# Last network of a four-stage kernel: seven block products for eight in two of four column blocks, and rows kept in DRAM

## Chip, cores, metric

One core of a Trainium2 chip. The metric is device time in microseconds (us) of one execution; several runs are made and the median is taken. Engines: PE (TensorE; PEld is its weight load), DVE (VectorE), ACT (ScalarE), POOL (GpSimd), SP (its queue issues most of the DMAs).

## What is computed

x is 8 x 256 rows of 512 values in float32. Four stages, each added to x: a long convolution over heads, a first gated network with 8-bit activations and ternary weights (hidden width 1408), an attention over the context, and a last gated network with 8-bit activations in groups of 64 and 1-bit weights (hidden width 2048). Cut to the two networks:

```python
def _bitlinear(x, w):                      # first network: one scale per row
    return jnp.einsum('bsi,oi->bso', _activation_quant(x), _weight_quant(w))
...
def _quant_weight_1b(w):                   # last network
    return _ste(w, jnp.sign(w) * jnp.mean(jnp.abs(w)))
def _quant_act(x):                         # groups of 64
    xg = x.reshape(shp[:-1] + (shp[-1] // GSIZE, GSIZE))
    s = jnp.clip(jnp.max(jnp.abs(xg), axis=-1, keepdims=True), EPS, None)
    q = jnp.round(jnp.clip(xg * (QB / s), -QB, QB)) * (s / QB)
    return _ste(x, q.reshape(shp))
def _bitlinear(x, w):
    return _quant_act(x) @ _quant_weight_1b(w).T
h = jax.nn.silu(_bitlinear(x, w1)) * _bitlinear(x, w2)
return _bitlinear(h, w3)
...
x = x + jnp.tanh(g_ffn[0]) * _L0_ffn_ref(_layernorm(x), ...)
x = x + jnp.tanh(g_xattn[1]) * _L1_xattn_ref(_layernorm(x), ctx_2048, ...)
x = x + jnp.tanh(g_ffn[1]) * _L1_ffn_ref(_layernorm(x), ...)
```

## The kernel before

The 2048 rows are 16 row tiles of 128 (`NT`), kept in SBUF as `xs`. Every engine works its instructions off in the order in which they are written: the program is under a manual schedule, so a step that waits holds up all that stands behind it on the same engine or queue.

*Convolution* (line 349 and around it, heads in a loop of 32): PE with float32 matmuls, DVE and POOL form products; `job(h, slot, ...)` hangs other work on the heads. Statistics for the layer normalisation of the first row tiles of the next stage are such jobs (`first_by_act`).

*First network* (loop over `t`, lines 861 to 1040): per row tile three column blocks of up products (`up_block`, L861), SiLU on ACT, a gate on DVE, then the row maximum (`row_max`), integers on ACT (`i8h`, L1018), clipping on POOL (`qh`, L1036), a transposing DMA (`hqT`, L1038), and two tiles later the 11 down products (`down0`, L878). `ln_finish` turns the statistics of four tiles into a reciprocal root on DVE and POOL; the group of the tiles 4 to 7 is done at `t == 1` (`FINISH[0]`). `odd_back` (L990, L991) adds what the convolution left over.

*Attention* (loop over `t` with `masked`, `readout`): PE float32, and SP loads keys, values and the last network's weights, of which ACT takes the signs.

*Last network.* The weights are +1 and -1 in `w1q[0]`, `w1q[1]` (512 x 2048 each) and `w1q[2]` (2048 x 512). An activation tile is split into a rounded part `hi` (ACT, L1163) and the rest `lo` (DVE, L1168), both fp32r, and both are multiplied. Per row tile, four column blocks of 512: `up_products` does 16 matmuls of 128x128 by 128x512 (two weights, hi and lo, four chunks of 128), then SiLU on ACT and the gate on DVE (`up_gate`, L1201). Two column blocks make a half of 1024 (`half_quantised`): group maximum (L1116), scale and reciprocal (L1128, L1130), a 32x32 transpose of the scales (L1329) and their way to DRAM (`d`, L1331), the integers `times` (L1135), their transposing DMA (`qT`, L1352), and the scales spread over the partitions from DRAM (`sT`, L1339, two issues). `hidden_high` then forms v = qT * sT on DVE (L1373) and its `hi`; `low` its `lo`. `down` does 32 matmuls a row tile (L1383), one row tile behind the up products. `front_turned` prepares the next row tile in the same way (normalisation L196, maximum, integers, DMAs, and v at L1433); `finish` adds the result to `xs` (L228) and stores it (L1396). Four PSUM banks take the up products in turn (`ps_mm`), two the down products (`ps_o`).

Of the kernel before, what the change touches and what calls it, by code (L numbers as in the profile page):

```python
# [13 lines left out]
I16 = mybir.dt.int16  # L14
# [28 lines left out]
def flamingo_gated_kernel(  # L43
# [65 lines left out]
    gw = const.tile([P, 2], F32, name="gw")  # L109
    gw0, gw1 = gw[:, 0:1], gw[:, 1:2]  # L110
# [534 lines left out]

    means = ((25, "act2"), (26, "act2"), (28, "act2"), (29, "act"))
# [228 lines left out]
    def down0(hqT):  # L875
        po = ps_o.tile([P, L], F32, tag="o", name="po")
        for c in range(NF0):
            nc.tensor.matmul(  # L878
                po, hqT[:, c, :], w0q[2][:, c, :], start=(c == 0), stop=(c == NF0 - 1)
            )  # L880
        return po


    natural = list(range(NT))
# [8 lines left out]
        0: (st0, 1, "0"), 4: (st0, 2, "0"), 8: (st0, 3, "0"),  # L893
# [103 lines left out]
    for t in range(NT + 1):  # L997
# [3 lines left out]
        if new and t > 0 and t != 2:  # L1001
            front_norm(t + 2)
# [11 lines left out]
        if t in (0, 2):  # L1014
            front_norm(t + 2)
        if 1 <= t:
            q = p1.tile([P, FF0], I8, tag="i8h", name="i8h")
            nc.scalar.activation(q, h_.pop(t - 1), AF.Copy, scale=sc)  # L1018
# [15 lines left out]
        if 1 <= t:  # L1034
            b = p2.tile([P, FF0], BF16, tag="qh", name="qh0")
            nc.gpsimd.tensor_scalar(b, q, 127.0, -128.0, ALU.min, ALU.max)  # L1036
            bT = p_hq.tile([P, NF0, P], BF16, tag="hqT", name="hqT")
            nc.sync.dma_start_transpose(out=bT, in_=b)  # L1038
            f3 = small.tile([P, 1], F32, tag="f3", name="f3")
            nc.gpsimd.tensor_scalar(f3, inv, gw0, None, ALU.mult)  # L1040
            hq_[t - 1] = (bT, f3)
# [8 lines left out]
        if t == 1:  # L1050
            ln_finish(*FINISH[0])
# [70 lines left out]
    def scales(v, n, tag, back=None):  # L1122

        back = group_max(v, n, tag, back)
        return back, to_8_bits(back, tag)

    def to_8_bits(back, tag):
        nc.vector.tensor_scalar(back, back, Q_EPS, 1.0 / 127.0, ALU.max, ALU.mult)  # L1128
        r = small.tile([P, back.shape[-1]], F32, tag="gr" + tag, name="gr")
        nc.vector.reciprocal(r, back)  # L1130
        return r
# [39 lines left out]
    def split(pool, v, tag):  # L1171
        return low(pool, v, high(pool, v, tag), tag)
# [27 lines left out]
    def up_gate(hh, pb, sl):  # L1200
        nc.vector.scalar_tensor_tensor(  # L1201
            hh, pb, wmean1[:, 1:2], sl, op0=ALU.mult, op1=ALU.mult
        )

    SIGNS = [2, 2, 2, 2, 2, 2, 2, 2, 2, 2, 1, 1, 1, 1]
    BY_POOL = set(range(4, NT))
    e_, r_ = {}, {}
    signs = [(0, make) for make in signs]  # L1210
    for t in range(NT + 2):
# [71 lines left out]
        if t == NT:  # L1283
            mean_w1(2)
            nc.vector.tensor_scalar(gw1, wmean1[:, 2:3], gate_f[1], None, ALU.mult)
# [8 lines left out]
        if t == NT - 2:  # L1294
            times(xn4, q, back)
        if t == NT - 1:
            ln_some(st4, natural, GRP, "4")
            hh = px.tile([P, FF1 // 2], F32, tag="hh", name="hh4")
# [10 lines left out]
    with ExitStack() as ph:  # L1309
        p2 = pool(ph, "p4", 2, reuse_waits="tile")  # L1310
        p3 = pool(ph, "p4three", 3, reuse_waits="tile")
        pk = pool(ph, "p4keep", 1, reuse_waits="tile")

# [7 lines left out]
        p1 = pool(ph, "p4one", 1, reuse_waits="tile")  # L1321
        NB = FF1 // 512
        HW = FF1 // 2
        HC, HG = HW // P, HW // GS

        def squares(back, tag):

# [9 lines left out]

# [6 lines left out]
        def half_quantised(hh, k):  # L1344

            back = backs["h", k]
            r = scales(hh, HW, "h", back[:, :HG])[1]
            d = squares(back, "h")
            q = p2.tile([P, HW], I16, tag="qh", name="qh")
            times(q, hh, r)  # L1350
            qT = p3.tile([P, HC, P], I16, tag="qT", name="qT4")
            nc.sync.dma_start_transpose(out=qT, in_=q)  # L1352
            sT = p3.tile([P, HC, P], F32, tag="sT", name="sT")
            spread_rows(sT, d, HC)
            return qT, sT

        def front_turned(t):

            back = backs["x", t % 2]
            xn, q = front(t, back[:, : L // GS])[:2]  # L1360
            d = squares(back, "x")
            qT = pk.tile([P, NL, P], I16, tag="xT", name="xT4")
            nc.sync.dma_start_transpose(out=qT, in_=q)
            sT = pk.tile([P, NL, P], F32, tag="xsT", name="xsT")
            spread_rows(sT, d, NL)
            return xn.rearrange("p (c m) -> p c m", m=P), qT, sT

        def hidden_high(halves, f):

            qT, sT = halves[f // 2]  # L1370
            c = slice((f % 2) * NL, (f % 2 + 1) * NL)
            v = p2.tile([P, NL, P], F32, tag="v", name="v4")
            nc.vector.tensor_tensor(v, qT[:, c, :], sT[:, c, :], ALU.mult)  # L1373
            return v, high(p1, v, f"h{f}")

        def hidden_parts(halves, f):
            return low(p1, *hidden_high(halves, f), f"h{f}")

        def down(po, hT, blocks):
            for b in blocks:  # L1380
                for c in range(NL):
                    for k in range(2):
                        nc.tensor.matmul(  # L1383
                            po,
                            hT[b][k][:, c, :],
                            w1q[2][:, b * NL + c, :],
                            start=(b == 0 and c == 0 and k == 0),
                            stop=(b == NB - 1 and c == NL - 1 and k == 1),
                        )

        def new_out():
            return ps_o.tile([P, L], F32, tag="o", name="po4")

        def finish(t, po):
            residual(t, po, gw1)
            nc.sync.dma_start(out=out[t * P : (t + 1) * P, :], in_=xs[:, t, :])  # L1396

        first, second = range(NB // 2), range(NB // 2, NB)
        prev, sums = None, []
        for t in range(NT):
            last = t == NT - 1
            for s in sums:
                finish(*s)
            sums, hT, high_ = [], [], {}
            if 0 < t < NT - 1:
                nxt = front_turned(t + 1)
            if t > 0:  # L1410
                hh = px.tile([P, HW], F32, tag="hh", name="hh4")
                g = up_products(xT, 0)
                if prev is not None:
                    high_ = {f: hidden_high(prev, f) for f in first}
                up_gate(hh[:, 0:512], *g)
                hT += [low(p1, *high_[f], f"h{f}") for f in first if f in high_]
                g = up_products(xT, 1)
                if prev is not None and not last:
                    high_ = {f: hidden_high(prev, f) for f in second}
                up_gate(hh[:, 512:1024], *g)  # L1420
            halves = [half_quantised(hh, 0)]
            if prev is not None and not last:
                hT += [low(p1, *high_[f], f"h{f}") for f in second]
            hh = px.tile([P, HW], F32, tag="hh", name="hh4")
            g = up_products(xT, 2)
            if t == 0:
                turned = front_transposed(xn4)
            up_gate(hh[:, 0:512], *g)
            if t == 0:
                nxtT = split(pk, turned, "x1")  # L1430
            g = up_products(xT, 3)
            if 0 < t < NT - 1:
                nc.vector.tensor_tensor(*nxt, ALU.mult)  # L1433
            if t + GRP + 1 < NT:
                ln_some(st4, natural, t + GRP + 1, "4")
            up_gate(hh[:, 512:1024], *g)
            if 0 < t < NT - 1:
                nxtT = split(px1, nxt[0], "x")
            xT = nxtT
            halves.append(half_quantised(hh, 1))  # L1440
            if 0 < t < NT - 1:
                po = new_out()
                down(po, hT, first if t == NT - 2 else range(NB))
                if t < NT - 2:
                    sums.append((t - 1, po))
                else:
                    begun = (po, hT)
            if last:
                po, hT0 = begun
                down(po, hT0, second)  # L1450
                hT += [hidden_parts(prev, f) for f in second]
                finish(t - 2, po)
                po = new_out()
                down(po, hT, range(NB))
                hT = [hidden_parts(halves, f) for f in range(NB)]
                finish(t - 1, po)
                po = new_out()
                down(po, hT, range(NB))
                finish(t, po)
            prev = halves  # L1460
# [47 lines left out]
```

## Time and profile before

| | |
|---|---|
| runs | 727.43, 728.82, 724.93 us; median 727.43 |
| profiled execution | 726.16 us, span 724.3, mean granted clock 0.995 |
| PE | 3200 instructions; up products of the last network: pa and pb, hi and lo, x256 each, 389 to 392 ns from start to modelled end |
| last network | from about 368 us to the end |
| last matmul, then residual and store | residual starts at 720.40 |
| DMA | 99.36 MB, mean 137 GB/s |

PE's matmuls are pipelined: the time from the start of one to the start of the next is shorter than the duration that a row shows. Where an engine waited, a line ends in brackets: how long it was idle, and what ended that.

### The profile page before, as it was taken

How to read it: one execution, taken by the hardware profiler on the slowest of the kernel's cores; microseconds unless marked ns; L12 is line 12 of the kernel's file. 1: busy time of each engine (PE TensorE's matmuls, PEld its weight loads, DVE VectorE, ACT ScalarE, POOL GpSimd, SP SyncE). 2: the span in 40 equal slices, each digit the busy share in tenths (PEclk: the TensorE clock that was granted, in tenths of full speed). 3: DMA queues.
4: the chain of work that ended last, by engine and by line, in shares of the span. 5: the costliest groups of instructions: out<-in, count | busy, mean ns of one | idle time of the engine just before them, and what ended most of it. 6: DMA issues, size and time to landing. Idle time of an engine off the chain costs nothing.

```text
span 724.3 us, 10121 instructions
## 1 busy us (share of the span) xinstructions
PE 711.4 (98%) x3200; PEld 531.6 (73%) x3200; DVE 598.5 (83%) x1224; ACT 367.4 (51%) x664; POOL 264.2 (36%) x371
## 2 busy tenths in 40 slices
PE   7999999999989999999999999999999999999997
PEld 6777777777544444657678888888888888888885
DVE  5699888999788887877877988988888988777965
ACT  5577887879787777757742222332222332212322
POOL 4798998989885535545400020000200002000000
PEclk8999999999999999999999999999999999999999
DMA  6675586921246566698605654454544454544443
GB/s 197 227 230 173 186 280 187 303 67 44 43 82 140 145 140 171 150 275 259 206 1 101 123 119 100 96 117 91 126 104 98 98 117 92 125 105 100 95 90 87
DMA packets 149970, 99.36 MB, mean 137 GB/s; under 512 B 83806, under 2 KB 127838, under 8 KB 149918
## 3 DMA queue, kind: packets, MB, share of 16 engines
q1 hardware_dynamic: 149608, 98.38, 52.3%
q0 software_dynamic: 256, 0.26, 0.6%
q8 instruction: 25, 0.41, 0.2%
q14 instruction: 27, 0.22, 0.1%
q10 hardware_dynamic: 54, 0.08, 0.1%
HBM read 75.58 MB, written 5.03 MB: 111 GB/s over the span
## 4 chain that ended last, share of the span: by engine, by line
PE 91%; DVE 2%; DMA 2%; POOL 2%; issue 1%; ACT 1%; SPq 0%; DVEq 0%; ACTq 0%; POOLq 0%
PE y L349 22%; PE po L1383 16%; PE pb L1189 15%; PE pa L1189 15%; PE po L878 5%; PE pa L861 4%; PE pb L861 4%; PE po L981 4%; PE ps L952 3%; PE tr L416 1%; PE tr L941 1%; DMA hqT<-qh 1%; DMA sT<-d 1%; DMA ch<-in_ctx_heads 1%; POOL xs L991 0%
## 5 line engine op out<-in xcount | busy, mean ns | idle before, releaser
L349 PE MATMUL y<-kv,toep 128*128 128x288 f32 x640 | 160.8, 408 | 0.7 <-ACT qx L313 0.6
L349 PEld LDWEIGHTS y<-kv,toep 128*128 128x128 f32 x640 | 119.9, 191 | 33.1 <-ACT qx L313 0.8
L1197 ACT ACTIVATE sl<-pa,wmean 128x512 f32<-128x512 f32 x64 | 44.0, 688 | 195.3 <-PE pa L1189 195.3
L1383 PE MATMUL po<-w,lo 128*128 128x512 f32 x256 | 99.9, 390 | 0.0
L1383 PE MATMUL po<-w,hi 128*128 128x512 f32 x256 | 99.6, 389 | 0.0
L181 POOL TENSOR_TENSOR nwt<-rstd 128x4 f32<-128x4 f32 x33 | 6.5, 198 | 242.2 <-DVE rstd L176 240.5
L326 POOL TENSOR_TENSOR kv<-cx 128x1024 f32<-128x1024 f32 x32 | 60.6, 1894 | 24.1 <-ACT cx L313 23.9
L1189 PE MATMUL pa<-w,hi 128*128 128x512 f32 x256 | 69.2, 392 | 0.0
L1189 PE MATMUL pb<-w,hi 128*128 128x512 f32 x256 | 68.6, 390 | 0.1
L1189 PE MATMUL pa<-w,lo 128*128 128x512 f32 x256 | 68.4, 389 | 0.0
L1189 PE MATMUL pb<-w,lo 128*128 128x512 f32 x256 | 68.4, 389 | 0.0
L394 POOL TENSOR_TENSOR prod<-prod 128x1024 f32<-128x1024 f32 x28 | 66.3, 2368 | 0.0
L861 PEld LDWEIGHTS <-xqT 128*128 128x128 bf16 x384 | 37.5, 98 | 37.8 <-issue 0.5
L1163 ACT CAST hi<-v 128x512 fp32r<-128x512 f32 x64 | 39.1, 622 | 48.2 <-DVE v L1373 48.1
L1201 DVE SCALAR_TENSOR_TENSOR hh<-pb,wmean,sl 128x512 f32<-128x512 f32 x64 | 47.7, 746 | 14.7 <-PE pb L1189 14.6
L1383 PEld LDWEIGHTS po<-w,lo 128*128 128x128 f32 x256 | 48.1, 188 | 10.9 <-DVE lo L1168 1.0
L1189 PEld LDWEIGHTS pa<-w,hi 128*128 128x128 f32 x256 | 47.8, 188 | 10.7 <-ACT hi L1163 0.6
L1189 PEld LDWEIGHTS pb<-w,hi 128*128 128x128 f32 x256 | 48.0, 188 | 10.5 <-DVE hh L1201 0.6
L1189 PEld LDWEIGHTS pa<-w,lo 128*128 128x128 f32 x256 | 48.1, 188 | 10.1
L1189 PEld LDWEIGHTS pb<-w,lo 128*128 128x128 f32 x256 | 48.1, 188 | 10.0
L1383 PEld LDWEIGHTS po<-w,hi 128*128 128x128 f32 x256 | 48.1, 188 | 9.9
L371 DVE TENSOR_TENSOR prod<-y,qx 128x512 f32<-128x512 f32 x64 | 43.7, 683 | 8.5 <-ACT y L359 4.4
(163 smaller groups left out, 1341.7 us busy)
## 6 DMA issues: line engine op xcount, KB each, us to landing
sT<-d SPq DMA_DIRECT2D x64, 256.0 KB
toep<-ssm_skip SPq DMA_DIRECT2D x31, 256.0 KB
ch<-in_ctx_heads SPq DMA_DIRECT2D x32, 128.0 KB
w1a<-in_L_w1t SPq DMA_DIRECT2D x8, 512.0 KB
w1a<-in_L_w2t SPq DMA_DIRECT2D x8, 512.0 KB
w1st<-in_L_w1t SPq DMA_DIRECT2D x16, 256.0 KB
w1st<-in_L_w2t SPq DMA_DIRECT2D x16, 256.0 KB
cT<-in_ctx_t SPq DMA_DIRECT2D x8, 512.0 KB
```

The source lines that it names most:

```text
L326: nc.gpsimd.tensor_tensor(kv[:, :, 0 : ND * HD].rearrange("p a (i d) -> p a i d", d=ND), cx[:, :, 0:HD].unsqueeze(3).to_broadcast([P, NL * ...
L349: nc.tensor.matmul(y[:, k, :, W0 : W0 + NPAIR], toeps[h][:, d * P : (d + 1) * P], kvs[h][:, mi * B : (mi + 1) * B, :].rearrange("p b n -> ...
L371: nc.vector.tensor_tensor(prod[:, 0, r, :, :], yv[:, :, W0 : W0 + ND * HD].rearrange("p a (i d) -> p a i d", d=ND), view(q, [HX, n], [1, H ...
L394: nc.gpsimd.tensor_tensor(flat[0], flat[0], flat[1], ALU.add)
L861: nc.tensor.matmul(pp[:, :fw], xqT[:, c, :], w0q[i][:, c, f0 : f0 + fw], start=(c == 0), stop=(c == NL - 1),)
L878: nc.tensor.matmul(po, hqT[:, c, :], w0q[2][:, c, :], start=(c == 0), stop=(c == NF0 - 1))
L981: nc.tensor.matmul(po, eT[:, c, :], cN[:, c, :], start=(c == 0), stop=(c == S // P - 1))
L1163: nc.scalar.copy(hi, v)
L1189: nc.tensor.matmul(pp, xT[k][:, c, :], w1q[i][:, c, f0 : f0 + 512], start=(c == 0 and k == 0), stop=(c == NL - 1 and k == 1),)
L1197: nc.scalar.activation(sl, pa, AF.Silu, scale=wmean1[:, 0:1])
L1201: nc.vector.scalar_tensor_tensor(hh, pb, wmean1[:, 1:2], sl, op0=ALU.mult, op1=ALU.mult)
L1383: nc.tensor.matmul(po, hT[b][k][:, c, :], w1q[2][:, b * NL + c, :], start=(b == 0 and c == 0 and k == 0), stop=(b == NB - 1 and c == NL - ...
```

## The change

In the last network, row tiles from 2 on are taken in pairs. For the first two of the four column blocks (`NS = 2`), the products of the pair's two row tiles with both weights are done as one 2 x 2 block product: the rows of the block matrix are the two row tiles, its inner index is the two halves of the 512 inputs (`KH = 2` chunks), its columns are the two weights. Seven block products of 4 matmuls (`plan_crossed`) take the place of eight, with four sums of activations (`sum_rows`, POOL, split into hi and lo again) and four combined weight forms for each column block (`t1` to `t4`, POOL, made once; `t1` in place of the second weight's first half). The seven results are put together on ACT, DVE and POOL. The other two column blocks are done as before (`plan_gated`).

Work is now cut into units of two hidden blocks of 512: a crossed unit has the same column block of both row tiles, a gated unit two column blocks of one row tile. A pair is two crossed and two gated units; down products of a unit (16 matmuls) follow the own products of the unit two later. `at(u, n, f)` gives each step a place in the order, `n` being counted in matmuls of unit `u`, and a sort by place writes all out.

The old row values are kept in DRAM (`kept`) and fetched twice, for the normalisation and for the residual; `xs` is used as scratch. Normalisation moves to POOL (`apply_row`); statistics of the row tiles 8 to 15 to ACT, those of 4 to 7 into the attention. A `v` or a `lo` is one step of 1024, or two halves on POOL and DVE (`low_part`). The second weight's mean moves from the gate into the last factor `gw1` and the clipping threshold (`eps_h`).

In the first network, integers, clipping and transposing DMA of a tile are cut in two (`CUTS`), and the statistics of the tiles 4 to 7 are finished in the convolution's last step with a Sqrt on ACT (`second_sqrt`, `second_inverse`).

```diff
+    def second_sqrt():
+        std = small.tile([P, GRP], F32, tag="nwv", name="std")
+        nc.scalar.activation(std, st0[1][:, :, 1], AF.Sqrt, bias=ln_eps)
+        st0[1] = (st0[1], std)
...
+    job(31, "act", second_sqrt)
+    job(31, "dve", second_inverse)
...
-        0: (st0, 1, "0"), 4: (st0, 2, "0"), 8: (st0, 3, "0"),
+        4: (st0, 2, "0"), 8: (st0, 3, "0"),
...
-            nc.gpsimd.tensor_scalar(b, q, 127.0, -128.0, ALU.min, ALU.max)
-            bT = p_hq.tile([P, NF0, P], BF16, tag="hqT", name="hqT")
-            nc.sync.dma_start_transpose(out=bT, in_=b)
+            for o, sl in zip(bT, CUTS):
+                nc.gpsimd.tensor_scalar(b[:, sl], q[:, sl], 127.0, -128.0, ALU.min, ALU.max)
+                nc.sync.dma_start_transpose(out=o, in_=b[:, sl])
...
+        def combine(o, a, b, op):
+            nc.gpsimd.tensor_tensor(o, a.bitcast(F32), b.bitcast(F32), op)
...
+        def sum_rows(a):
+            va, vb, s = rows4[a], rows4[a + 1], sums_
+            s1, s2, s3, s4 = (s[:, k * KH : (k + 1) * KH, :] for k in range(4))
+            k0, k1 = slice(0, KH), slice(KH, NL)
+            nc.gpsimd.tensor_tensor(s1, vb[:, k0, :], vb[:, k1, :], ALU.add)
+            nc.gpsimd.tensor_tensor(s2, s1, va[:, k0, :], ALU.subtract)
+            nc.gpsimd.tensor_tensor(s3, va[:, k0, :], vb[:, k0, :], ALU.subtract)
+            nc.gpsimd.tensor_tensor(s4, va[:, k1, :], s2, ALU.subtract)
...
+        def low_part(u, *engs):
+            hi, lo = hT_[u]
+            n = HC // len(engs)
+            for k, eng in enumerate(engs):
+                c = slice(k * n, (k + 1) * n)
+                eng.tensor_tensor(lo[:, c], v4[:, c], hi[:, c].bitcast(F32), ALU.subtract)
...
+        def plan_crossed(u):
...
+            for n, (k, pair, w) in enumerate((
+                (1, lambda: part(a, 0), b11[f]), (6, lambda: sum_part(2), t2[f]),
+                (5, lambda: sum_part(1), b12[f]), (2, lambda: part(a, 1), b21[f]),
+                (7, lambda: sum_part(3), t3[f]), (4, lambda: part(b, 1), t4[f]),
+                (3, lambda: sum_part(4), b22[f]),
+            )):
+                at(u, NL * n, product, u, k, pair, w)
+            dve, pool_ = nc.vector, nc.gpsimd
+            at(u, 4, copied)
+            at(u, 8, lambda: add(dve, u2, y(6), s_[1]))
+            at(u, 12, lambda: nc.scalar.copy(second, y(5)))
+            at(u, 15, lambda: add(pool_, first, u2, second))
+            at(u, 16, lambda: add(dve, s_[1], y(2), s_[1]))
+            at(u, 19, lambda: silu(s_[1], s_[1]))
+            at(u, 20, lambda: add(dve, u3, y(7), u2))
+            at(u, 23, lambda: add(pool_, second, u3, second))
+            at(u, 24, fourth)
+            at(u, 27, lambda: silu(s_[4], s_[4]))
+            at(u, 28, lambda: add(dve, first, y(3), first))
+            at(u, 30, lambda: add(pool_, second, second, s_[4], ALU.mult))
+            at(u, 31, lambda: add(dve, first, first, s_[1], ALU.mult))
+            return 28
...
+            if u < NU - 1:
+                at(u, n, largest, u)
+                at(u, n + 5, inverse, u)
+                at(u, n + 13, integers, u)
+                at(u, n + 18, spread4, u)
...
+                at(u, n + 8 if u > 1 else n - 1, value, u - 1)
+                m = max(n + 8 if u > 1 else n, begins[u + 1] - begins[u] if u < NU - 1 else 0)
+                at(u, m + 6, high_part, u - 1, places.get(u - 1, hl))
+                both = u < NU - 2 and paired[u + 1]
+                fast = u >= NU - 2 or u == 1 or u % 4 == 2
+                engs = (nc.gpsimd, nc.vector) if both else (nc.vector if fast else nc.gpsimd,)
+                at(u, m + 10, low_part, u - 1, *engs)
...
+        def plan_rows(u, n):
+            at(u, 9, value_row, n + 1)
+            at(u, 9, sum_rows, n)
+            at(u, 15, hi_row, n)
+            at(u, 18, hi_row, n + 1)
+            at(u, 20, lo_row, n)
+            at(u, 23, lo_row, n + 1)
+            at(u, 23, hi_sums)
+            at(u, 26, lo_sums)
```

## The prediction

> **What bounds the kernel now.** I read the busy shares first, then busy time by stretch, then the chain of waits in the last network, then single instructions on a time line.
>
> ```profile
> PE 711.4 (98%) x3200; PEld 531.6 (73%) x3200; DVE 598.5 (83%) x1224; ACT 367.4 (51%) x664; POOL 264.2 (36%) x371
> ```
> ```profile
> 378.00:401.00 23.00, 22.87 (x103) 18.56 (x102) 19.14 (x35) 6.87 (x11) 0.00 (x0) 1.00 0.42 88
> 401.00:683.00 282.00, 282.00 (x1246) 233.59 (x1245) 239.65 (x437) 75.81 (x118) 12.60 (x42) 1.00 0.50 107
> ```
> Columns of the stretches: length, busy PE, PEld, DVE, ACT, POOL, granted clock, DMA share, GB/s. From 401 to 683 us PE never rests; DVE works 239.65 of 282 us (85%), POOL 12.6 (4%). PE is the bound, with DVE 15% below it.
>
> ```profile
> 422.37 7.25 PE po L1383 x32
> ...
> 442.32 1.81 PE pb L1189 x8
> 444.13 2.04 PE po L1383 x9
> ```
> Chain of waits, start and length: from one group of down products to the next, 444.13 - 422.37 = 21.76 us go by, with 64 up and 32 down matmuls in them: 0.2267 us each. So a pair of row tiles costs PE 192 x 0.2267 = 43.5 us, and DVE 0.85 x 43.5 = 37.0.
>
> ```profile
> 424.73 0.68 DVE L1168 TENSOR_TENSOR lo<-xn,hi 128x512 fp32r<-128x512 f32 x1
> 424.80 0.66 POOL L183 TENSOR_SCALAR nwt<-nwt 128x4 f32<-128x4 f32 x1
> ...
> 427.07 1.23 DVE L1135 TENSOR_TENSOR qh<-hh,gr 128x1024 int16<-128x1024 f32 x1
> 427.22 1.14 POOL L182 TENSOR_TENSOR nwt<-nwt,nwv 128x4 f32<-128x4 f32 x1
> ```
> Time line, start and length: two POOL instructions of 128x4 elements. Their median over the whole trace is 0.19 and 0.20 us. Here they last 0.66 and 1.14, until 0.05 us after the DVE instruction beside them is over. Both DVE instructions read two operands from SBUF. Beside the reduction L1116 (one operand) POOL's steps kept their 0.20. So POOL stands still while DVE reads two SBUF operands. The reverse shows once:
>
> ```profile
> 15.15 1.89 POOL L326 TENSOR_TENSOR kv<-cx 128x1024 f32<-128x1024 f32 x1 [0.89 <-ACT cx L313]
> 16.65 0.68 DVE L706 TENSOR_SCALAR xnp<-xs,rstd,nmr 128x512 f32<-128x512 f32 x1
> 17.00 0.64 POOL L332 TENSOR_TENSOR kv<-ch 128x128 f32<-128x128 f32 x1
> ```
> The DVE step takes 0.68 where its like, L196, takes 0.54 (x16), and ends 0.29 after POOL's ends; the POOL step behind it takes 0.64 where its median is 0.46. In the last network the kernel hardly uses POOL, so today this costs nothing.
>
> **The change part by part.**
>
> *Matmuls.* In the changed program's order, 7 pairs x 2 crossed units issue 28 matmuls in place of 32: 56 fewer, up products 968 for 1024. 56 x 0.2267 = 12.7 us, if PE stays the bound. A pair then costs PE 184 x 0.2267 = 41.7.
>
> *First network.* Two PE waits are there:
> ```profile
> PE po L878 <- DMA hqT<-qh: 1.2, 1, 1.2
> PE tr_back L424 <- ACT back L990: 0.8, 1, 0.8
> ```
> The second hangs on ACT, which had idled 3.40 us at L201 for POOL's L187, the end of the statistics that move to the head of the convolution's last step. The first hangs on a transposing DMA issued at 209.92; with the tensor cut in two, its first part leaves some 1.3 us earlier (half of ACT's 1.46 and of POOL's 1.36). Gain 2.0; bounds 0 and 2.6 (two more small waits of 0.4 and 0.35 near 314 and 318). What it adds per tile, one more transposing DMA (1.4 us of SP) and some 0.2 us fixed cost on ACT and on POOL, lies under PE's 7.1 us a tile: ACT is busy 24 of 30 us there, POOL 14. Without that cover it would be 16 x 0.2 = 3.2. The Sqrt and the reciprocal for four tiles (0.29 and 0.15) lie under the convolution's matmuls.
>
> *DVE per pair of row tiles.* Removed: 4 gates at 0.745 (3.0); the two normalisations, now on POOL, at 0.54 (1.1); statistics of 10 in 13 tiles, now on ACT or earlier, at 0.87 (1.3); 8 subtractions for "lo" at 0.68 become two halves and one of 1024 elements (1.22 by L1135), 2.9 less; 8 "v" of 512 become 4 of 1024, 0.5 less. Added: 12 element-wise steps of 512 at 0.68 (L371, from PSUM), 8.2; the low part of the sums, 1.2. Net +0.6; overlap of neighbours (0.07 each) brings it to about +0.3. DVE needs 37.3 of PE's 41.7: 89%, before any wait.
>
> *POOL per pair.* Six products or sums of 512 at 1.04 (L408) to 1.27 (L991), two "lo" halves and one of 1024 (1.89 by L326 to 2.37 by L394), two normalisations at 0.77 (L933), four quarter sums at 0.66 (L409): about 15 us where it had almost none. No bound by itself, but now POOL and DVE stand in each other's way, and DVE, in order, waits for POOL's results:
> - After each crossed unit the group maximum needs POOL's last product. POOL still has 2 x 1.27 to do after DVE's third sum, plus 0.4 behind a two-operand DVE step and 0.15 of handing over: 3.1; DVE fills 1.9 of it. Idle 1.2, twice: 2.4.
> - The two halves of "lo" start together, one behind the other: 0.4, twice: 0.8.
> - The low sums wait for four POOL sums (2.64), 1.6 behind the DVE steps "lo" and 2 x "lo row", and ACT's copy (1.05): 5.3, of which DVE fills 3.0. Idle 2.3.
> - One "times" of a row behind POOL's "lo" of 1024: 0.5.
> - DMA: an sT took 5.2 us from issue to use where DVE waited for it (391.30 to 396.48); in the new order the second crossed unit's and the row's come about 1.0 and 0.6 too late.
>
> Sum 7.6; 37.3 + 7.6 = 44.9 us a pair: DVE with its waits, not PE, sets the pace. 44.9 - 43.5 = +1.4, seven times: +9.8. Bounds: no waits, PE's 41.7, -12.7 in all; POOL at its slow rows and sT at 6.4 us (429.67 to 436.08): waits 11, 48.3 a pair, +33.
>
> *Start.* Eight weight forms on POOL (1.9 to 2.37 each) fall beside units 1 to 3. Also only four column blocks, not six, now stand on PE before the first down products. Walked with these rows, unit 0's operands are just in time; unit 1's last comes at 406.4, where PE wants it at 404.5: 1.9. DVE's three two-operand steps on unit 0's way may each meet a form; for the three I take 1.6 in all. +3.5; bounds 0 and 8 (all three meeting 2.37 less a margin of 0.9).
>
> *End.* The last four groups of down products come at DVE's pace; its lag in one pair is 44.9 - 41.7 = 3.2. I take +2, bounds 0 and 5. After PE's last matmul (720.4) the residual and the store are as before.
>
> *Covered.* Rows kept in DRAM: 16 writes and 30 reads of 256 KB, 12 MB on 99; DMA share 0.50 in this stage leaves room; on SP some 46 issues of about 0.5 us. In SP's order each fetch waits on a row buffer released a unit before; behind it stand qT and sT, for which "v" on DVE waits; a late fetch is bounded by the 6.4 us above. ACT's six statistics (2.1 us each: two passes and their small steps) lie under 45 us in which ACT is mostly idle (6.87 of 23 before); without cover up to 12.8.
>
> Sum on the profiled execution (span 724.3, 726.2 in all): 726.2 - 2.0 + 9.8 + 3.5 + 2.0 = 739.5. The runs' median, 727.4, is 1.3 above that execution, so about 740.
>
> The Trainium skill, "SBUF — State Buffer", section "SBUF: two separate sides", calls the port pair of DVE and GpSimd an exclusive lock for a whole instruction, and this for DVE steps with two SBUF inputs too. The rows show POOL held by such steps, and DVE held only by the one of L706. If DVE were never held, as a narrow reading of the rows allows, its 1.3 us in the second and fourth item would go: 43.6 a pair, about 730.5; with the rule it is the sum above.
>
> **Rivals.**
> - *PE stays the bound* (faster). The waits shrink under 4 us a pair: hand-overs or DMA quicker than the rows, POOL at 1.04. For it: DVE has 4.4 us left in a pair by busy time alone. Against: the held POOL rows. 726.2 - 12.7 - 2.0 + 2 = 713.5, about 715.
> - *Gain and loss cancel* (no change). Waits of about 5.5: 42.8 a pair, -5; with start and end 5.5 and the first network -2: about 725, 726 on the median.
> - *POOL's chain stretches further* (much slower): POOL at 1.27 and 2.37 and sT at 6.4: +33 + 8 + 3 - 2, near 769. It decides once the waits pass 8 us a pair.
> - *The saving is not there*: excluded by the 56 missing instructions of the same width.
>
> **How the numbers follow.** Slower as worked out, 0.50 (own range 731 to 756); much slower 0.11; no change 0.10; faster 0.29. Half a per cent (3.6 us) is about what these runs can tell from none. Slower 0.61, same 0.10, faster 0.29. The range 714 to 757 leaves out the far slow case and the best of the fast one.
>
> **What would show it.** DVE near 90% busy and PE idle at crossed units, waiting for DVE; POOL adds far above 1.04 beside L-lines that subtract or multiply two SBUF tensors; DVE waiting for POOL at the group maximum; 0.2267 a matmul as before; the two waits of the first network gone. I am wrong if PE is dense in the pairs (184 matmuls in 41.7 us), or if PE waits for DMA rather than DVE.

## The result and the profile after

The changed kernel takes 774.61 us (median of four runs, 773.73 to 775.81), the kernel before 726.75 beside it: ratio 1.066, 95% interval 1.064 to 1.069. Slower was forecast, but by 13 us and not by 48; the range ended at 757. The busy shares of the changed kernel, then its stretches of the last network (length, busy PE, PEld, DVE, ACT, POOL, clock, DMA share, GB/s):

```profile
PE 724.0 (94%) x3131; PEld 524.9 (68%) x3144; DVE 640.0 (83%) x1194; ACT 400.8 (52%) x741; POOL 429.0 (56%) x488
```
```profile
376.46:416.37 39.91, 32.91 (x134) 25.80 (x133) 32.66 (x40) 20.42 (x57) 22.10 (x12) 0.91 0.46 101
...
465.95:708.48 242.53, 222.38 (x923) 171.15 (x921) 203.16 (x303) 68.90 (x95) 106.62 (x91) 0.99 0.54 116
708.48:773.00 64.52, 54.05 (x217) 41.90 (x215) 43.24 (x65) 15.49 (x21) 14.90 (x10) 0.94 0.40 97
```

The middle line is five pairs, from the first crossed product of one to that of the sixth: 48.5 us each where PE needs 41.7 and the kernel before took 43.5. PE, which never rested, is idle 20 us of 242; POOL went from 4% to 44%, DVE from 85% to 84%. The first line is the way to the first crossed product: 128 matmuls, 29.0 us by 0.2267, take 40.5 (PE starts at 375.90, 0.56 before that stretch). The last is the last pair and the end: 216 matmuls and the old tail of 3.9 are 52.9 us; it takes 64.5. Losses against a dense PE are so 11.5 at the start, 41.9 in the six pairs between (416.37 to 708.48 less 6 x 41.7), 11.6 at the end; the kernel before lost 2.1 (346.99 us from 377.31 on, against 1504 x 0.2267 + 3.9). Less these 2.1, the 12.7 saved and 1.4 by which the network starts earlier, the losses are the 48.7 by which the span grew. PE's list of waits has only 7.0 of the 11.5 at the start and 6.5 of the 11.6 at the end; the granted clock of these two stretches was 0.91 and 0.94, against 0.99 in the five pairs.

What DVE waited for in five pairs, from 469.70 to 712.10 (us in total, times, longest):

```profile
DVE slo L1512 <- ACT shi L1509: 12.0, 5, 2.4
DVE xs L1536 <- DMA xs<-d: 6.2, 4, 2.0
DVE gam_h L1140 <- POOL hh L1625: 5.9, 5, 1.2
DVE gam_h L1140 <- POOL xs L1625: 5.9, 5, 1.2
DVE xn L1490 <- DMA xs<-d: 3.8, 5, 0.9
```

These sum to 33.8, 6.8 a pair, close to what was foreseen place by place: 1.2 twice for POOL's last product (foreseen: the same), 2.4 for the sums of rows (2.3), 2.0 for scales (1.6). What had not been sized is on the time line:

```profile
570.44 1.28 POOL L1547 TENSOR_TENSOR hlo<-xs,hhi 128x512 fp32r<-128x512 f32 x1 [7.08 <-ACT hhi L1540]
570.93 1.34 DVE L1547 TENSOR_TENSOR hlo<-xs,hhi 128x512 fp32r<-128x512 f32 x1
...
592.21 2.39 POOL L1547 TENSOR_TENSOR hlo<-xs,hhi 128x1024 fp32r<-128x1024 f32 x1 [2.73 <-ACT hhi L1540]
592.73 1.90 DVE L1147 TENSOR_SCALAR gam_x<-gam_x 128x8 f32<-128x8 f32 x1
```

DVE's half of `lo` starts 0.49 after POOL's, takes 1.34 where 0.68 is usual, and ends 0.55 after POOL's half has ended. A DVE step of eight elements a row takes 1.90, where the same step for the pair's other row (at 597.48) takes 0.17: it ends with POOL's `lo` of 1024. In both places POOL had begun first and kept its time. The time stands in DVE's busy column, so no list of waits shows it.

### The profile page after: what moved, and what is told of

It reads as the page before. It is cut to its first block, busy times and chain, and to the rows that moved or that the text cites. A ratio compares the mean times of both kernels' runs of the same rounds, so it can differ in the third digit from the quotient of the medians.

```text
span 773.0 us, 10418 instructions
## 1 busy us (share of the span) xinstructions
PE 724.0 (94%) x3131; PEld 524.9 (68%) x3144; DVE 640.0 (83%) x1194; ACT 400.8 (52%) x741; POOL 429.0 (56%) x488
## 4 chain that ended last, share of the span: by engine, by line
PE 45%; DVE 24%; DMA 9%; issue 8%; POOL 6%; ACT 4%; SPq 1%; DVEq 0%; POOLq 0%; ACTq 0%
PE y L350 17%; DMA xs<-d 5%; PE pa L878 5%; PE pb L878 5%; PE po L896 4%; DVE xs L1154 4%; PE po L1557 4%; DMA d<-sq 3%; PE y L1524 3%; DVE gam_h L1140 3%; PE po L1001 2%; DVE xs L1625 2%; PE ps L972 2%; DVE gam_x L1147 2%; DVE sl L1625 2%
## 5 line engine op out<-in xcount | busy, mean ns | idle before, releaser
L1557 PE MATMUL po<-w,hlo 128*128 128x512 f32 x232 | 68.2, 418 | 15.0 <-DVE hlo L1547 15.0
L1557 PE MATMUL po<-w,hhi 128*128 128x512 f32 x232 | 67.4, 414 | 7.3 <-ACT hhi L1540 5.0
L1557 PEld LDWEIGHTS po<-w,hlo 128*128 128x128 f32 x232 | 45.0, 199 | 30.4 <-DVE hlo L1547 18.5
L1557 PEld LDWEIGHTS po<-w,hhi 128*128 128x128 f32 x232 | 44.8, 196 | 20.8 <-ACT hhi L1540 6.1
L1524 PE MATMUL pab<-w,xhi 128*128 128x512 f32 x176 | 54.3, 390 | 0.0
L1524 PE MATMUL pab<-w,xlo 128*128 128x512 f32 x176 | 54.3, 389 | 0.0
L1536 DVE TENSOR_TENSOR xs<-xs 128x1024 f32<-128x1024 int16 x31 | 37.0, 1194 | 18.3 <-DMA xs<-d 13.9
L878 PE MATMUL pa<-w,xqT 128*128 128x512 bf16 (+1 forms) x187 | 45.6, 361 | 0.6 <-ACT sl L886 0.3
L878 PE MATMUL pb<-w,xqT 128*128 128x512 bf16 (+1 forms) x190 | 45.8, 361 | 0.1
L896 PE MATMUL po<-w,hqT 128*128 128x512 bf16 x170 | 40.0, 379 | 0.3
```

The lines of the kernel that those rows point to most:

```text
L878: nc.tensor.matmul(pp[:, :fw], xqT[:, c, :], w0q[i][:, c, f0 : f0 + fw], start=(c == 0), stop=(c == NL - 1),)
L896: nc.tensor.matmul(po, part, w0q[2][:, c, :], start=(c == 0), stop=(c == NF0 - 1))
L1524: nc.tensor.matmul(pp, pair[k][:, c, :], w[:, c, :], start=start and k == c == 0, stop=stop and k == 1 and c == KH - 1,)
L1536: nc.vector.tensor_tensor(v4, qT_[u % 2], sT_[u % 2], ALU.mult)
L1557: nc.tensor.matmul(po_[t], o[:, b * NL + c, :], w1q[2][:, f * NL + c, :], start=(n == 1 and c == k == 0), stop=(n == NB and c == NL - 1 an ...
```

## The experiments

**1. Both engines side by side.** Behind the last store of the kernel before, six like steps on each engine, alone and together:

```diff
+        for dve, pool_ in ((dd, None), (dp, None), ..., (None, qq), ..., (dd, qq), (dp, qq), ...):
+            meet()
+            for _ in range(6):
+                if dve:
+                    dve()
+                if pool_:
+                    pool_()
```

> The kernel before, with a row of measurements behind its last store: six like steps on DVE alone, six on POOL alone, then both kinds begun together, for several kinds of DVE step (two operands from SBUF; one from PSUM; one operand with per-row factors; one operand with constants; a reduction; 8 elements a row with a constant and with a per-row factor) beside a POOL sum of 128x512 and beside a POOL scaling of one operand. Theory (POOL and DVE hold each other): alone 0.68 (DVE sum) and 1.04 to 1.27 (POOL sum); together six of each take the sum of both, about 6 x 1.9 = 11.5 us, each engine's rows stretched to about 1.9; the reduction keeps its time beside POOL; 8 elements with a per-row factor are held like the 1.90 at 592.73 us of the changed kernel's trace. Rival (the steps run side by side, only in-order waits cost): together as long as the slower engine alone, 6 x 1.27 = 7.6 us, DVE's rows at 0.68.

The time line of that kernel; x6 is one group of six. L1494 is POOL's sum; on DVE L1473 adds two SBUF tensors, L1476 one from PSUM and one from SBUF, L1479 scales one with per-row factors, L1485 reduces, L1491 is eight elements with a per-row factor:

```profile
724.15 4.32 DVE L1473 TENSOR_TENSOR xs<-xs 128x512 f32<-128x512 f32 x6
...
734.21 3.46 DVE L1479 TENSOR_SCALAR xs<-xs 128x512 f32<-128x512 f32 x6
...
751.65 1.56 DVE L1491 TENSOR_SCALAR xs<-xs 128x8 f32<-128x8 f32 x6
...
768.39 9.16 DVE L1473 TENSOR_TENSOR xs<-xs 128x512 f32<-128x512 f32 x6
...
769.08 9.59 POOL L1494 TENSOR_TENSOR xs<-xs 128x512 f32<-128x512 f32 x6
...
779.20 4.31 DVE L1476 TENSOR_TENSOR xs<-bank,xs 128x512 f32<-128x512 f32 x6
...
779.48 7.97 POOL L1494 TENSOR_TENSOR xs<-xs 128x512 f32<-128x512 f32 x6
...
787.98 7.68 DVE L1479 TENSOR_SCALAR xs<-xs 128x512 f32<-128x512 f32 x6
...
806.51 7.48 DVE L1485 TENSOR_REDUCE xs<-xs 128x16 f32<-128x1024 f32 x6
...
824.09 6.93 DVE L1491 TENSOR_SCALAR xs<-xs 128x8 f32<-128x8 f32 x6
```

Alone, POOL's six sums take 7.96 (753.95 to 761.91). Together with DVE's two-operand sums (4.32 alone) both are over after 10.28 (768.39 to 778.67), where the sum is 12.28 and side by side would be 7.96. So nearly one after the other, a little less than expected. The held kinds are those with two SBUF operands, and also scalings of one operand (3.46 to 7.68) and tiny steps (1.56 to 6.93). A step that reads one operand from PSUM and a reduction keep their time to 0.01 us, and POOL beside them takes 7.97. Scalings and tiny steps with constants are held as well (2.73 to 7.57, 1.20 to 3.13). Beside POOL's scaling of one operand the holding is weaker: DVE's sums take 6.05, its scalings with per-row factors 4.61. The rival falls.

The Trainium skill, "SBUF — State Buffer", section "SBUF: two separate sides", names two SBUF inputs and the fast modes as what contends, with the loser fully blocked. The two-operand rows agree in kind, though not in full: 16% of the sum was overlapped.

**2. All units gated.** No crossed products, and so no sums of rows and no weight forms; all else as changed:

```diff
-            UNITS += [[(t, f), (t + 1, f)] for f in range(NS)]
-            UNITS += [[(t + k, f), (t + k, f + 1)] for k in range(2) for f in range(NS, NB, 2)]
+            UNITS += [[(t + k, f), (t + k, f + 1)] for k in range(2) for f in range(0, NB, 2)]
...
-            at(u, 9, sum_rows, n)
```

> The changed kernel with all units gated: no sums of rows, no weight forms, eight block products again; units, places, rows kept in DRAM, the low part on POOL and the first network stay as changed. Theory (what crossed units add on POOL and DVE is the loss): PE sets the pace again, 43.5 us a pair; POOL keeps the three low parts of 1024 and two normalisations, about 9 us a pair, but DVE has fewer steps and slack; 726.2 - 2.0 + 1 to 8 at the start = 725 to 732. Rival (units of two blocks, rows in DRAM and 12 MB more traffic are the loss): stays above 750. DVE's busy time per pair falls under 36 in both.

736.88 us, ratio 1.013 (1.010 to 1.017): a little above the range, far under the rival's. Crossed products cost the 38 us between this and 774.6; the rest of the change (units, places, rows in DRAM, normalisation and part of the `lo` on POOL) costs 10. Some 4 of these have an odd cause. PE never waited in the pairs, and yet one took 44.3 us for 192 matmuls (409.40 to 675.22 is six), not 43.5. Matmuls by their weights and activations:

```profile
L1524 PE MATMUL pab<-w,xhi 128*128 128x512 f32 x265 | 81.9, 390 | 0.0
...
L1557 PE MATMUL po<-w,hlo 128*128 128x512 f32 x195 | 53.4, 396 | 0.0
L1557 PE MATMUL po<-w,hhi 128*128 128x512 f32 x192 | 52.6, 396 | 0.0
L1524 PE MATMUL pab<-w,hi 128*128 128x512 f32 x128 | 40.2, 395 | 0.0
```

Same shape, type and clock, 390 or 396 ns by the tile that is read. Run 5 and run 6 take this up.

**3. POOL's steps left out, and 4. moved to DVE.**

```diff
-            at(u, 15, lambda: add(pool_, first, u2, second))
...
+                if eng is nc.gpsimd:
+                    continue
```
```diff
-            dve, pool_ = nc.vector, nc.gpsimd
+            dve, pool_ = nc.vector, nc.vector
...
-            nc.gpsimd.tensor_scalar(rows4[t], rows4[t], rstd[:, c], nmr[:, c], ALU.mult, ALU.add)
+            nc.scalar.activation(rows4[t], rows4[t], AF.Identity, bias=nmr[:, c], scale=rstd[:, c])
```

> The changed kernel without POOL's two-operand steps in the pairs: the two sums and the product of a crossed unit, the four sums of rows and POOL's shares of the low parts are left out (not moved), so the output is not the reference's. Weight forms and normalisation stay. Theory (DVE's own steps are held by POOL): DVE's busy time per pair falls from 40.6 to about 37.3 and its waits for POOL go; PE comes near its 41.7; a pair takes 42 to 43.5, the whole about 725 to 738. Rival (waits alone): DVE's busy time stays at 40.6, only about 3.6 us of waits a pair go: about 45 a pair, 748 to 755. Rival (DMA): the waits of DVE for transfers grow into the room: over 46 a pair, above 755.

> The changed kernel with those steps of POOL moved to DVE (sums and product of the crossed units, sums of rows, all low parts) and the normalisation moved to ACT: POOL does nothing in the pairs. Theory (a POOL step of two operands costs DVE its time anyway): DVE at its own pace 37.3 + 6 x 0.68 + 2.4 + 4 x 0.36 = 45.2 busy a pair, with waits for ACT and DMA of 2 to 3: 47 to 48.5 a pair, 765 to 777, as fast as with POOL's help. Rival (POOL takes work off DVE and only the waits cost): 40.6 + 7.9 + 3.5 = 52 a pair, about 799.

Left out: 730.49 us, ratio 1.004 (1.003 to 1.006). Five pairs of that kernel, same columns as above:

```profile
459.92:671.84 211.92, 211.92 (x921) 172.70 (x920) 189.44 (x308) 69.98 (x95) 12.68 (x24) 1.00 0.59 133
```

42.4 a pair, PE dense, DVE 37.9: the prediction's own 37.3 was about right for a DVE that is hardly held. The 44 us by which this is under 774.6 all hang on POOL's steps, by holding and by the waits for their results together; this run does not part the two.

Moved to DVE: 766.45 us, ratio 1.053 (1.050 to 1.056). Five pairs there:

```profile
468.92:702.89 233.97, 219.19 (x921) 174.96 (x920) 220.48 (x368) 76.54 (x105) 4.84 (x14) 0.98 0.54 120
```

46.8 a pair, DVE busy 44.1. POOL does 21 us of work a pair in the changed kernel, and the kernel is 8 us faster without that help, with DVE doing its steps (and ACT the normalisation, which POOL did). POOL did spare DVE some work: DVE's busy time a pair is 40.6 with that help and 44.1 without, where the steps add 6.2 to run 3's 37.9. But DVE's waits and gaps are 7.9 a pair with it (48.5 less 40.6) and 2.7 without. The Trainium skill, "Perfetto Trace Analysis", section "Optimizing Scalar/DVE Operations", warns that moving work between these two engines might not help; here it hurt.

**5 and 6. The shift of 32 bytes undone**, in the changed kernel and in the gated one:

```diff
-    gw = const.tile([P, 2], F32, name="gw")
-    eps_h = const.tile([P, 1], F32, name="eps_h")
-    gw0, gw1 = gw[:, 0:1], gw[:, 1:2]
+    gw = const.tile([P, 3], F32, name="gw")
+    gw0, gw1, eps_h = gw[:, 0:1], gw[:, 1:2], gw[:, 2:3]
```

> The changed kernel with eps_h as a third column of gw and not a tile of its own. A tile of 4 bytes a partition takes 32, and all tiles placed behind it moved by 32 bytes: in the program's addresses 792 of the 1480 matmuls with the last network's weights now read a weight tile and an activation tile whose addresses differ by 32 modulo 64, where before none did. In the run with POOL's steps left out (PE never waits in the pairs) exactly the matmuls of hi, lo, hhi, hlo go at 0.2335 us each, those of xhi, xlo, shi, slo at 0.2267. Theory (the shift slows them): all at 0.2267; 792 x 0.0068 = 5.4 us less PE work; here, where DVE sets the pace in part of the time, 1 to 5 us less than 774.6: 769 to 774. Rival (the activations' tiles are slower for another reason, their place in a pool or the writer): 0.2335 stays, no change.

> The kernel with gated units only, with the same edit. PE sets the pace there (no wait of PE in the pairs, 44.0 to 44.4 us each for 192 matmuls). Theory (the shift): 43.5 us a pair, 768 slow matmuls x 0.0068 = 5.2 us less: about 731.5. Rival: 736.9 as without the edit.

The gated kernel falls to 732.99, ratio 1.007 (1.004 to 1.009), 43.5 us a pair (411.50 to 672.62 is six), and its slow rows are gone:

```profile
L1556 PE MATMUL po<-w,hlo 128*128 128x512 f32 x200 | 53.5, 389 | 0.0
L1556 PE MATMUL po<-w,hhi 128*128 128x512 f32 x196 | 52.4, 389 | 0.0
L1523 PE MATMUL pab<-w,hi 128*128 128x512 f32 x128 | 39.4, 389 | 0.0
```

So the placement is the cause, and a tile of four bytes cost some 0.6%. In the changed kernel the matmuls of `hi` and `lo` speed up as well (395 to 389), but nothing is won: 777.38, ratio 1.067 (1.064 to 1.070) against 1.066. I had expected 1 to 5 us; a pair still takes 48.7 (468.00 to 711.58 is five), so PE's own pace did not count there.

**7. No weight forms, and 8. scales spread early.**

```diff
-            (1, 0, make_t3, 0), (1, 10, make_t2, 0), (1, 30, make_t4, 0),
...
+            t3[f], t2[f], t4[f] = b22[f], b11[f], b21[f]
```
```diff
-                at(u, n + 18, spread4, u)
+                at(u, n + 12, spread4, u)
...
-                at(u0 + 2, 24, spread_row, n)
-                at(u0 + 2, 36, spread_row, n + 1)
+                at(u0 + 2, 10, spread_row, n)
+                at(u0 + 2, 21, spread_row, n + 1)
```

> The changed kernel without the eight weight forms: plain blocks of the weights stand in their place, so the output is not the reference's. Pairs stay as they are. Theory (forms on POOL hold DVE's two-operand steps at the start): the first crossed product comes 5 to 8 us earlier after the start of the last network (40.4 us now, 33.4 with gated units only), 767 to 770 in all. Rival (the start is late for the transfers and the smaller cover, forms fall beside DVE's other work): under 2 us, 772 to 775.

> The changed kernel with the spreading of scales (two issues on SP) placed ahead of the transposing DMA of the integers for hidden units, and right behind the row's own steps for the rows. Rival theory (transfers of scales that come late are a main part of the loss): DVE's waits for DMA, 1.9 us a pair, go: 7 x 1.9 = 13 us less, about 761. Theory (POOL and DVE holding each other): DVE has the same work; the waits shrink but the chain through POOL stays: 0 to 6 us less, 768 to 775; if SP waits for the scales' landing ahead of the transposes, these come later and nothing is won.

Without forms 768.47, ratio 1.055 (1.052 to 1.058): the first crossed product comes 34.3 us after the network's start (375.07 to 409.34), not 40.5; the first pair takes 46.5 for 49.6, and from the second on the pairs keep about 48.8 (455.80 to 699.61 is five). So forms on POOL cost 6 us of the 11.5 at the start. The profiled execution, 764.95, is the fastest of the four; by the median the whole gains 6.1.

Spread early: 765.94, ratio 1.052 (1.050 to 1.054), between the two expectations. DVE's waits over nearly the same stretch:

```profile
DVE slo L1512 <- ACT shi L1509: 9.6, 4, 2.4
DVE xn L1490 <- DMA xs<-d: 8.5, 5, 2.1
DVE gam_h L1140 <- POOL hh L1625: 5.9, 5, 1.2
DVE gam_h L1140 <- POOL xs L1625: 5.9, 5, 1.2
```

The hidden units' wait for scales (6.2) is gone, the rows' grew from 3.8 to 8.5, and a pair takes 48.0 (513.00 to 704.85 is four), 0.6 less than the same four in the changed kernel. Most of the gain is outside the pairs: 36.1 instead of 40.5 to the first crossed product, 59.5 from the last pair's start to the end instead of 64.5. (In this execution the last network began 3.6 us later than in the changed kernel's, at 379.48, so these gains sum to more than the whole.) So late transfers cost most at the start and the end; why is not shown.

**9. Sums beside the kernel before**, which nothing waits for:

```diff
+        def beside(t):
+            if t > 5:
+                for _ in range(2):
+                    nc.gpsimd.tensor_tensor(xs[:, 2, :], xs[:, 0, :], xs[:, 1, :], ALU.add)
...
             g = up_products(xT, 3)
+            beside(t)
```

> The kernel before, with eight POOL sums of 128x512 (rows of xs that are already stored, results unused) put beside each row tile of the last network from tile 6 on, two behind each column block; nothing waits for them. Theory (each POOL step of two operands takes its time from DVE's two-operand steps beside it, wanted or not): DVE has 18.5 us of work in a tile of 21.76; about 55% of it is of the kind that is held; 8 x 0.55 x 1.1 = 4.9 us more: 23.4 a tile, DVE becomes the bound, 10 tiles x 1.6 = 16 us more: 735 to 750, with lo, v, times at a mean of 0.8 to 1.0 and the gate and the reduction as before. Rival (only waits for results cost time): 727, no row of DVE changes.

754.86 us, ratio 1.039 (1.036 to 1.042): 28 us for 80 sums whose results are never read. More than expected; I had reckoned with 1.1 for POOL's sum, which took 1.55. DVE's rows from 520 to 700 us, first three of the kernel before, then those of this one:

```profile
L1168 DVE TENSOR_TENSOR lo<-v,hi 128x512 fp32r<-128x512 f32 x34 | 21.8, 683 | 0.0
L1373 DVE TENSOR_TENSOR v<-qT,sT 128x512 f32<-128x512 int16 x34 | 21.6, 676 | 0.0
L1135 DVE TENSOR_TENSOR qh<-hh,gr 128x1024 int16<-128x1024 f32 x17 | 20.8, 1225 | 0.0
...
L1373 DVE TENSOR_TENSOR v<-qT,sT 128x512 f32<-128x512 int16 x28 | 34.7, 1278 | 0.4 <-DMA sT<-d 0.4
L1168 DVE TENSOR_TENSOR lo<-v,hi 128x512 fp32r<-128x512 f32 x28 | 30.6, 1132 | 0.0
L1135 DVE TENSOR_TENSOR qh<-hh,gr 128x1024 int16<-128x1024 f32 x14 | 22.8, 1626 | 0.0
L1201 DVE SCALAR_TENSOR_TENSOR hh<-pb,wmean,sl 128x512 f32<-128x512 f32 x28 | 20.7, 740 | 0.0
L1116 DVE TENSOR_REDUCE gam_h<-hh 128x16 f32<-128x1024 f32 x14 | 17.0, 1214 | 0.2
```

`v`, `lo` and the integers stretch from 676, 683 and 1225 ns; the gate, which reads PSUM, and the reduction stay at their 746 and 1216 or a little under. No dependency was added, so this is holding alone.

**10. The first network's part alone** on the kernel before (its hunks of the diff as they stand):

> The kernel before with the change's first-network part alone (integers, clipping and transposing DMA in two parts; statistics of the tiles 4 to 7 finished in the convolution's last step). By the term of the prediction: 2.0 us less, bounds 0 and 2.6: 724.7 to 727. In the changed kernel's trace the two PE waits of 1.2 and 0.8 are gone, and the last network began 0 to 1 us earlier than before. Rival: the ACT and SP work that it adds shows elsewhere and nothing is won.

726.78 us, ratio 0.999 (0.998 to 1.000): 0.4 us, if anything: the interval reaches none. PE's waits from 195 to 378 us of that kernel:

```profile
PE po L1000 <- ACT eT L994: 1.3, 1, 1.3
PE po L895 <- DMA hqT<-qh: 0.7, 1, 0.7
PE tr L960 <- ACT xn L201: 0.3, 1, 0.3
```

One wait (ACT `back`) is gone, one halved, and the attention's first down product waits 1.3 for ACT where it waited 0.4: 2.3 in all against 2.8.

**11. Three edits together** (4, 5 and 8):

> The changed kernel with three edits together: POOL's steps in the pairs on DVE (normalisation on ACT), scales spread early, the shift undone. If the three add: 766.5 - 8.7 - up to 5 = 753 to 758. DVE then needs about 44 us a pair without a wait, over PE's 41.7, so it stays slower than before in either theory; a rival in which waits are all that matters would put it near 735.

766.38, ratio 1.053 (1.052 to 1.055): no faster than run 4. With DVE alone the early spread made the rows' scales late (`xn` waits 14.4 us over six times). Why SP's order turns against it there was not tried.

**12. POOL's steps left out and the shift undone** (3 and 5):

> The kernel without POOL's two-operand steps in the pairs (left out, not moved; the output is not the reference's), with the shift of 32 bytes undone as well. PE never waited in its pairs with the shift (42.4 us each). Theory (the seven products are worth what the sum said once PE paces, and the shift cost 792 x 0.0068 = 5.4): 41.7 us a pair, 730.5 - 5 = 725 to 726.5, that is about 12 us lost at the start and the end against 12.7 saved. Rival (another limit of PE at 0.230 a matmul): 42.4 a pair, 730.

727.22, ratio 1.001 (0.999 to 1.002), a little over the range expected. Five pairs:

```profile
456.52:665.13 208.61, 208.61 (x921) 172.66 (x920) 188.54 (x307) 69.51 (x95) 12.25 (x24) 1.00 0.62 135
```

41.7 a pair, dense, 0.2267 a matmul: the saving of 12.7 is real, and here it is paid out. The total still only equals the kernel before, since 40.0 to the first crossed product (374.73 to 414.70) and 57.6 for the last pair and the end are 11.0 and 4.7 over their 29.0 and 52.9. With POOL's work in the pairs at no price at all, the change would have broken even.

## Why the prediction was wrong

*Right.* The saving (0.2267 a matmul, 41.7 a pair; run 12). DVE's own work without holding: 37.3 foreseen, 37.9 in run 3. DVE and not PE sets the pace (faster matmuls won nothing in run 5). The waits for results: 2.4 for POOL's last product (measured 2.4), 2.3 for the sums of rows (2.4), 1.6 for transfers (2.0).

*The step that failed* is the two small items of holding, "The two halves of `lo` start together, one behind the other: 0.4, twice: 0.8" and "One 'times' of a row behind POOL's 'lo' of 1024: 0.5": 1.3 a pair. I had looked for holding where two steps were sure to meet, and counted it as a wait. DVE's rows in the five pairs, two of the changed kernel and one of run 12, which leaves POOL's steps out:

```profile
L1547 DVE TENSOR_TENSOR hlo<-xs,hhi 128x512 fp32r<-128x512 f32 x10 | 13.3, 1335 | 0.0
L1147 DVE TENSOR_SCALAR gam_x<-gam_x 128x8 f32<-128x8 f32 x10 | 10.4, 1041 | 0.3
...
L1548 DVE TENSOR_TENSOR hlo<-xs,hhi 128x512 fp32r<-128x512 f32 x10 | 6.8, 684 | 0.0
```

DVE's half of `lo` takes 1.335 for 0.68, twice a pair: 1.3 where I had 0.8. Behind POOL's `lo` of 1024 stood not "times", which kept its 0.69, but the step of eight elements ahead of it (L1147): it takes 1.90 in one row of each pair and 0.17 in the other, which makes the mean of 1.04: 1.7 where I had 0.5. One low part of a row, which had no term, takes 1.23 for 0.68: 0.5. That is about 3.6 a pair where I had 1.3; DVE's other kinds of steps took what they take in run 3. DVE was busy 40.6, waited 6.8, and another 1.1 went mostly in gaps of under 0.15 between its steps, for which the sum had no term: 48.5 where I had 44.9. The difference, seven times, is 25 of the 35 us that were missed; 2.3 of its 3.6 are the holding, 1.1 the gaps, 0.5 the waits, less 0.3 of other work. Runs 1 and 9 show what the two items left out: a POOL step can take its time out of any DVE step of the held kind beside it, whatever waits for what. How much of POOL's work would meet such steps was not worked out from this, so a size that the rule would have given is not shown.

*POOL's work* was undersized with it: "about 15 us" a pair, measured 21.3. A sum of 512 took 1.53 to 1.64 where I had 1.04 to 1.27 (alone, in run 1, 1.33), and the four quarter sums 4.7 in all where I had 2.64. DVE's waits for these results still came out as foreseen: their terms had 0.4 and 1.6 for DVE steps ahead, which the 15 had not.

*The threshold on waits decided wrongly.* The much slower rival gave 48.3 a pair and 769, close to what came, but "once the waits pass 8 us a pair". Waits stayed at 6.8. That its price came close is luck: the stretch hid in busy time, and the start and the end lost more than it had.

*Start and end, +3.5 and +2.* The start lost 11.5 where I had 3.5 and a bound of 8: forms are 6 of it (run 7), early scales win some 4 (run 8). The last pair and the end lost 11.6 where I had 2 and the pair's 3.2: early scales win 5 there.

*First network, -2.0.* Alone it is worth 0.4 (run 10): one wait was replaced by another on ACT at the head of the attention. In the changed kernel the last network starts 1.4 earlier, in one execution; in the other runs that hold this part of the change it starts between 374.73 (run 12) and 379.48 (run 8), so the 1.4 tells nothing.

*Covered terms.* Rows in DRAM and units of two cost 5 us, not nothing (run 6, mostly PE's waits of 3.0 and 2.5 at the start and the end). The shift of 32 bytes was not seen at all; it cost the gated kernel 4 us and the changed one nothing that shows.

## What to carry to other kernels

Work that goes from DVE to POOL is not all taken off DVE: here POOL's 20 us of steps a pair spared DVE 3.5 us of busy time and brought 5 us of waits and gaps. What POOL's sums held were DVE's steps with two operands from SBUF, its scalings and its tiny steps; reductions and steps that read PSUM kept their time, so these are what to put beside POOL. Holding shows as longer busy rows, so compare the mean of each DVE row with its unheld like before trusting a list of waits. An algorithm that saves matmuls has to leave DVE a margin for its own sums, and its start and end are paid in full: in run 12 they alone ate the saving.

## Not expected of the hardware

- A DVE step of eight elements a row with a per-row factor took 6.93 for six beside POOL's sums, 1.56 alone; a reduction of 1024 elements took 7.48 in both cases.
- Both engines together took 10.28 for 12.28 of two-operand work: not fully one after the other.
- An fp32r matmul of 128x512 took 0.2335 us and not 0.2267 where its two SBUF tiles lay, by the program's addresses, 32 apart modulo 64 (run 2 against run 6, same clock of 1.00 in the pairs); equal remainders were fast, at 0 and at 32. In the kernel before, the first network's bf16 up products read tiles that differ in the same way and its down products tiles that do not; both show 379 ns.
